# Attention values in four column quarters, and softmax sums added up by POOL and DVE

## The chip, the cores and the metric

One core of a Trainium2 chip runs the kernel. The metric is device time in microseconds (us) of one execution. A core has a matrix engine (TensorE, PE in the profile, with its weight loads as PEld), three engines for elementwise work (VectorE, DVE; ScalarE, ACT; GpSimd, POOL), and DMA queues, which the SyncE queue (SP) feeds here. Each engine works through its own queue in order; the queues wait for each other by semaphores. The matrix engine writes to PSUM, eight banks of 128 partitions by 512 fp32 numbers.

## The reference

Four layers with residuals: a gated recurrence, a feed-forward layer, a differential attention, the feed-forward layer again. The change is in the attention. Inputs: 2 sequences of 1024 tokens, width 512; 16 heads of 32, each with two query sets on the same keys and values.

```python
x = x + _L0_attn_b_ref(_layernorm(x), Wq1, Wq2, Wk, Wv, Wlam, Wo)

def _L0_attn_b_ref(x, Wq1, Wq2, Wk, Wv, Wlam, Wo):
    q1, q2, k, v = (split_heads(x @ W) for W in (Wq1, Wq2, Wk, Wv))
    q = concatenate([q1, q2], axis=1)
    scores = einsum('bhqd,bhkd->bhqk', q, repeat(k, 2)) / sqrt(d)
    p = softmax(where(causal, scores, finfo.min), axis=-1)
    y = einsum('bhqk,bhkd->bhqd', p, repeat(v, 2))
    lam = sigmoid(x @ Wlam)
    return (y[:, :H] - lam * y[:, H:]) @ Wo
```

## The kernel before

The work before and after the attention (the recurrence, lines up to 413, and the two feed-forward layers, lines 500 to 556) is untouched. Everything below is in the attention stage.

**Pairs.** A pair `(b, g, p, par)` is two heads of sequence `b` that are worked on together; index `e` (0, 1) tells the two apart. There are 32 pairs, in groups of four with the same `b` and `g`. The 1024 queries of a sequence are two halves `qb` of 512 (`BLK`), that is eight tiles of 128 (`P`); the 1024 keys are eight blocks `kb` of 128.

**Units.** Under the causal mask a half needs key blocks 0 to 3 or 0 to 7: twelve units `(qb, kb)` per pair, numbered 0 to 11 (`units`). Units 0 to 3 are the first half, 4 to 11 the second. A unit with `kb >= 4*qb` is on the diagonal: it needs only the last `BLK - lo` queries, with `lo` 0, 128, 256 or 384.

**Six steps.** A pair runs in six steps of two units each. In step `t` of pair `n` the matrix engine's order, written out by hand (`manual_schedule` for PE alone), is:

- `weights_step` (units 2t and 2t+1): scores `t` = keys x queries, transposed so that keys are the partitions (L858, four matmuls), then a product of 3 rows with ones that adds minus the maximum (L865, four matmuls). ACT takes the exponential into the weights tile `pr` (L873, four buffers, both heads in one tile); POOL zeroes the masked triangle of a diagonal unit (`affine_select`, L876).
- `weigh` for the two units of the step before: the product of values and weights (L895), accumulated in the one PSUM bank outside the ring (`edge_bank`).
- work listed in `beside` for this step: projections of a later group (L717), transposes of the maxima, and around the change of sequence the values, the division by the sums and the output projection.
- `maxima_step` of the next pair: scores with queries as partitions (L798), to which DVE adds the causal mask (L804) and whose maximum it takes (L808). Both orders of the scores are needed, for the maxima must be known before the exponentials.

The maxima of a pair are split into three bf16 parts by POOL (`split_maxima`, L825 to L829: first half of the queries at step 2 of the pair before, second half at step 0 of the pair itself, after DVE has taken the smaller of two partial results, L822) and turned by PE (`turn_maxima`, L836, copied by DVE, L838) one step later.

Scores, projections and turned maxima share a ring of seven PSUM banks (`ring_bank`). The queues of DVE, ACT, POOL and SP are ordered by the framework's scheduler when the program is built; the matrix engine's is not.

**The product with the values.** Values are kept with 33 columns a head (`HV`): 32 numbers and a one, so that row 32 of the product is the sum of the weights. A product takes 64 columns (33 of use), so the two heads take the two halves of the array's columns:

```python
nc.tensor.matmul(
    y[64 * e : 64 * e + 64, lo:],
    all_values[:, HV * (NH * kb + h) : HV * (NH * kb + h) + 64],
    pr[:, e, : BLK - lo], start=(kb == 0), stop=last,
)
```

After the last unit of a half ACT copies the bank to `ys` (L912); SP sends 32 rows a head to `shares` and one row a head to `totals`. At the end of a sequence `divide` takes reciprocals of `totals` and `combine` multiplies them in; `project_out` follows.

**Loads.** Queries and keys go through DRAM scratch and come back as `qs` (1024 queries of one head, six buffers) and `ks`, loaded for pair n+2 at step 1 of pair n.

## Time and profile before

| | |
|---|---|
| three runs | 2176.17, 2178.66, 2180.66 us (median 2178.66) |
| profiled execution | 2177.11 us |
| its span | 2175.3 us |
| granted PE clock, mean | 0.995 |
| PE busy | 2122.4 us (98%) |
| DVE, ACT, POOL busy | 1126.2, 837.3, 448.1 us |
| attention stage, first to last L865 | 844 to 1767 us |
| product with the values, L895 | 1536 records, 291.6 us busy |

An fp32 product shows as two records. Busy time counts overlapped records once. Records of a matmul have modelled ends, so the cost of a group of matmuls is read from its start to the start of the next group. The profile gives, for each engine, busy time and what ended its idle time.

### The profile page before, as it was taken

What the parts mean: (1) busy time and instruction counts of PE and PEld (TensorE: products, weight loads), DVE (VectorE), ACT (ScalarE), POOL (GpSimd) and SP (SyncE); (2) the same over time, 40 slices, a digit from 0 to 9 for tenths busy, and PEclk for the clock granted to TensorE, in tenths of its full rate; (3) what the DMA queues carried; (4) which work ended last, traced back from release to release, by engine and by line L of the source; (5) the groups of instructions that cost most, each with busy time, mean ns of one, the idle gap of its engine ahead of it and who ended that gap; (6) DMA issues with size and microseconds to landing.
All of it is one profiled execution on the core that took longest, in us unless ns stands there. A gap on an engine that the chain in (4) does not pass through costs nothing.

```text
span 2175.3 us, 26073 instructions
## 1 busy us (share of the span) xinstructions
PE 2122.4 (98%) x9072; PEld 1273.5 (59%) x9072; DVE 1126.2 (52%) x2056; ACT 837.3 (38%) x1592; POOL 448.1 (21%) x808
## 2 busy tenths in 40 slices
PE   8999999999999999999999999999999999999998
PEld 3444444688888844555555454454545547888887
DVE  4767676533443235565656574565656763333322
ACT  4344343234334322343444332243434533343433
POOL 0312123122122220111111112121212221222222
PEclk9999999999999999999999999999999999999999
DMA  6111211600000144343434341244443223000000
GB/s 251 58 58 58 88 58 73 246 1 1 1 1 1 35 105 106 98 112 87 121 83 119 76 123 41 73 104 106 104 105 88 64 83 160 0 20 20 1 20 20
DMA packets 77874, 161.41 MB, mean 74 GB/s; under 512 B 19376, under 2 KB 27568, under 8 KB 77744
## 3 DMA queue, kind: packets, MB, share of 16 engines
q1 hardware_dynamic: 77744, 159.75, 25.1%
q8 instruction: 73, 1.20, 0.2%
q14 instruction: 57, 0.47, 0.1%
HBM read 109.08 MB, written 41.94 MB: 69 GB/s over the span
## 4 chain that ended last, share of the span: by engine, by line
PE 86%; DVE 4%; DMA 4%; ACT 2%; SPq 2%; issue 2%; POOL 0%; DVEq 0%; ACTq 0%; POOLq 0%
PE y L895 11%; PE g L511 11%; PE u L511 11%; PE f_out L532 11%; PE t L858 6%; PE s L798 5%; PE ag L260 5%; PE kv L260 5%; PE pq L717 4%; PE pq L260 3%; PE pv L689 3%; PE a_out L408 3%; PE b_out L956 2%; DMA qs<-sc 2%; PE t L865 2%
## 5 line engine op out<-in xcount | busy, mean ns | idle before, releaser
L873 ACT ACTIVATE pr<-t 128x512 f32<-128x512 f32 (+3 forms) x768 | 314.8, 497 | 368.6 <-PE t L865 364.8
L808 DVE TENSOR_REDUCE nmax<-s 128x1 f32<-128x512 f32 (+3 forms) x640 | 369.7, 627 | 54.6 <-PE s L798 54.5
L895 PE MATMUL y<-pr,val 128*64 128x512 f32 (+3 forms) x1536 | 291.6, 501 | 0.8 <-POOL maxima L827 0.8
L526 POOL TENSOR_TENSOR ssq<-ssq,sq 128x512 f32<-128x512 f32 x120 | 155.9, 1299 | 602.5 <-ACT sq L525 602.5
L517 DVE TENSOR_TENSOR h<-h,u 128x512 f32<-128x512 f32 x128 | 88.0, 688 | 362.5 <-PE u L511 356.4
L511 PE MATMUL g<-xs,w 128*128 128x512 f32 x1024 | 261.8, 397 | 0.9 <-ACT xs L461 0.7
L532 PE MATMUL f_out<-w,hs 128*128 128x512 f32 x1024 | 257.7, 394 | 0.3 <-DVE hs L520 0.3
L511 PE MATMUL u<-xs,w 128*128 128x512 f32 x1024 | 257.0, 393 | 0.0
L876 POOL TENSOR_SCALAR_AFFINE_SELECT pr<-pr 128x256 f32<-128x256 f32 x256 | 101.4, 408 | 593.6 <-ACT pr L873 593.3
L858 PE MATMUL t<-qs,ks 128*128 128x512 f32 (+3 forms) x768 | 198.4, 357 | 22.1 <-DVE parts L729 9.6
L511 PEld LDWEIGHTS u<-xs,w 128*128 128x128 f32 x1024 | 192.9, 188 | 43.6
L532 PEld LDWEIGHTS f_out<-w,hs 128*128 128x128 f32 x1024 | 191.6, 188 | 43.9 <-DVE hs L520 1.1
L804 DVE TENSOR_TENSOR s<-s,causal 128x128 f32<-128x128 f32 (+1 forms) x384 | 115.3, 336 | 195.3 <-PE s L798 195.3
L511 PEld LDWEIGHTS g<-xs,w 128*128 128x128 f32 x1024 | 190.5, 188 | 43.9 <-ACT xs L461 0.9
L798 PE MATMUL s<-ks,qs 128*128 128x512 f32 (+3 forms) x768 | 206.9, 391 | 6.2 <-DMA sc<-parts 3.9
L858 PEld LDWEIGHTS t<-qs,ks 128*128 128x128 f32 x768 | 139.2, 188 | 78.2 <-issue 20.8
L717 PE MATMUL pq<-b_xt,w_qk 128*128 128x512 f32 x384 | 175.8, 603 | 0.0
L519 ACT CAST hs<-h 128x512 fp32r<-128x512 f32 x128 | 79.4, 621 | 237.5 <-DVE h L517 237.5
L895 PEld LDWEIGHTS y<-pr,val 128*64 128x64 f32 x1536 | 93.3, 136 | 120.2 <-issue 86.1
L516 ACT ACTIVATE h<-g 128x512 f32<-128x512 f32 x128 | 76.6, 598 | 224.0 <-PE g L511 223.9
L798 PEld LDWEIGHTS s<-ks,qs 128*128 128x128 f32 x768 | 115.0, 190 | 69.4 <-issue 58.6
L520 DVE TENSOR_TENSOR hs<-h,hs 128x512 fp32r<-128x512 f32 x128 | 88.6, 692 | 83.1 <-ACT hs L519 83.1
(151 smaller groups left out, 2145.5 us busy)
## 6 DMA issues: line engine op xcount, KB each, us to landing
qs<-sc SPq DMA_DIRECT2D x128, 256.0 KB, 4.9
w<-w_kept SPq DMA_DIRECT2D x32, 768.0 KB, 8.9
sc<-parts SPq DMA_DIRECT2D x384, 64.0 KB, 1.7
ks<-sc SPq DMA_DIRECT2D x128, 128.0 KB, 4.0
w_kept<-w SPq DMA_DIRECT2D x16, 768.0 KB, 3.2
w<-in_w_gu_dram SPq DMA_DIRECT2D x32, 256.0 KB, 2.8
share<-ys SPq DMA_DIRECT2D x128, 64.0 KB, 2.0
w_in<-in_w_in_t_dram SPq DMA_DIRECT2D x5, 1024.0 KB, 11.0
```

The lines of the kernel that those rows point to most:

```text
L260: nc.tensor.matmul(po, w[:, k, ts(c, P)], xt[:, k, :], start=(k == 0), stop=(k == NKC - 1))
L511: nc.tensor.matmul(po, ws[f][:, part, ts(k, P)], xs[:, e, k, :], start=(k == 0 and e == 0), stop=(k == NKC - 1 and e == 1),)
L526: nc.gpsimd.tensor_add(ssq, ssq, sq)
L532: nc.tensor.matmul(po[j], hp[:, e, ts(j, P)], ws[f][:, 2, :], start=(f == 0 and e == 0), stop=(f == NF - 1 and e == 1),)
L717: nc.tensor.matmul(po, w[:, k, ts(kind, P)], xts[b][:, k, ts(e, BLK)], start=(k == 0), stop=(k == NKC - 1),)
L798: nc.tensor.matmul(po[:, x, :], qs[:, ts(j, P)], ks[:, first : first + nk], start=True, stop=True,)
L804: nc.vector.tensor_tensor(diagonal, diagonal, causal.unsqueeze(1).to_broadcast([P, len(heads), P]), ALU.add,)
L808: nc.vector.tensor_reduce(nmax[pair][:, first // BLK, j, heads[0] : heads[-1] + 1], po, AX.X, ALU.max, negate=True,)
L858: nc.tensor.matmul(banks[u, e][:, :nq], ks[:, ts(kb, P)], qs[:, q0 : q0 + nq], start=True, stop=False,)
L873: nc.scalar.activation(pr[:, e, :nq], banks[u, e][:, :nq], AF.Exp)
L876: nc.gpsimd.affine_select(out=pr[:, :, :P], in_=pr[:, :, :P], compare_op=ALU.is_ge, fill=0.0, base=0, pattern=[[0, 2], [1, P]], channel_mu ...
L895: nc.tensor.matmul(y[64 * e : 64 * e + 64, lo:], all_values[:, HV * (NH * kb + h) : HV * (NH * kb + h) + 64], pr[:, e, : BLK - lo], start= ...
```

## The change

**Quarters.** The two heads' products are split once more, by the parity `a` of the query tile: even tiles go to columns 64a + 32e with a = 0, odd ones with a = 1. Each product uses the 32 values of a head as weights and half of the query tiles as the moving side, so four products fill the four quarters of the array's columns, and the output has 256 columns in place of 512. A diagonal unit with d tiles masked leaves out tiles below d, and the last one (d = 3) has odd tiles only.

**Sums.** The column of ones is gone, and so is the padding. The sums of weights are added up elementwise over key blocks in an fp32 tile `acc` per half: units 5 to 8 of the second half (the ones with `lo` = 0 after the first) by POOL, one add of both heads' 1024 numbers a partition each; the units with `lo` > 0 by DVE (1, 2, 3 and 9, 10, 11), with a copy of 2 x 128 numbers at unit 1. Unit 0 and unit 4 are read where they are, as the first term. `add_up` then multiplies `acc` by a matrix of ones for four blocks at once (two heads of this pair's first half, two of the last pair's second half) into one ring bank, ACT copies it, SP sends four rows to `totals`. It stands at step 2 of a pair, and once more after the last.

**Loads.** `qs` is two tiles, one per half, with four and six buffers, loaded for pair n+2 at step 2 of pair n and at step 0 of pair n+1.

**Room and order.** Two instead of four buffers of `maxima`, three instead of four of `mt`; the second half's `combine` and the output projection around the change of sequence come up to two steps later.

```diff
-        all_values = b_d.tile([P, NQ * NH * HV + 64 - HV], F32, name="val")
+        val = b_d.tile([P, NQ, D], F32, name="val")
+        ones32 = b_c.tile([P, HD], F32, name="ones32")
...
-        def load_stacks(pair):
+        def load_stacks(pair, halves=range(2)):
             b, g, p, par = pair
-            for e in range(2):
-                if par == 0:
-                    load_stack(b, g, 2, 2 * p + e)
-                load_stack(b, g, par, 2 * p + e)
+            for half in halves:
+                for e in range(2):
+                    if par == 0 and half == 0:
+                        load_stack(b, g, 2, 2 * p + e)
+                    load_stack(b, g, par, 2 * p + e, half)
...
                 steps.append((pair, u, pr))
+                if kb == 0:
+                    first_pr = pr
+                    continue
+                if kb == 1:
+                    accs[pair, qb] = b_a.tile(
+                        [P, 2, BLK], F32, tag=f"acc{qb}", name=f"acc{name(pair)}_{qb}"
+                    )
+                acc = accs[pair, qb]
+                more = first_pr if kb == 1 else acc
+                other = nc.vector if lo else nc.gpsimd
+                if kb == 1 and lo:
+                    other.tensor_copy(acc[:, :, :lo], more[:, :, :lo])
+                other.tensor_add(acc[:, :, lo:], more[:, :, lo:], pr[:, :, :nq])
             return steps
+        def add_up(*blocks):
+            n_sums[0] += 1
+            po = ring_bank(f"sums{n_sums[0]}")
+            rows = slice(0, 64 * len(blocks))
+            for x, (pair, qb) in enumerate(blocks):
+                for e in range(2):
+                    nc.tensor.matmul(
+                        po[64 * x + 32 * e :][:32], ones32, accs[pair, qb][:, e, :],
+                        start=True, stop=True,
+                    )
+            sm = b_c.tile([P, BLK], F32, tag="sums", name=f"sm{n_sums[0]}")
+            nc.scalar.copy(sm[rows], po[rows])
...
         def weigh(pair, u, pr):
...
-            for e in range(2):
-                h = operands(pair, e)[2]
-                nc.tensor.matmul(
-                    y[64 * e : 64 * e + 64, lo:],
-                    all_values[:, HV * (NH * kb + h) : HV * (NH * kb + h) + 64],
-                    pr[:, e, : BLK - lo],
-                    start=(kb == 0), stop=last,
-                )
+            for a in range(2):
+                first = a if a >= d else a + 2
+                if first < d:
+                    continue
+                for e in range(2):
+                    h = operands(pair, e)[2]
+                    nc.tensor.matmul(
+                        y[64 * a + 32 * e :][:32, first // 2 * P : 2 * P], val[:, kb, ts(h, HD)],
+                        pr[:, e, :].rearrange("p (t q) -> p t q", q=P)[:, first - d : QB - d : 2, :],
+                        start=(kb == 0), stop=(d == 2 + a),
+                    )
...
             if n + 2 < len(pairs):
-                at(n, 1, load_stacks, pairs[n + 2])
+                at(n, 2, load_stacks, pairs[n + 2], (0,))
+                at(n + 1, 0, load_stacks, pairs[n + 2], (1,))
...
+            at(n, 2, add_up, (pair, 0), *([(pairs[n - 1], 1)] if n else []))
...
                         for c in range(NKC):
-                            at(n + 1, 2 + 2 * e + c // 2, combine, b, c, e)
+                            m, t = ((n + 1, 2 + c // 2), (n + 1 + c // 2, 5 * (c < 2)))[e]
+                            at(m, t, combine, b, c, e)
                     for j in range(NQ):
-                        m, t = (n + 1, 5) if j < 2 else (n + 2, (j - 2) // 3)
+                        m, t = (n + 1, 5) if j < 2 else (n + 2, j // 2 - 1)
                         at(m, t, lambda b=b, j=j: project_out(b, j, held["o", b]))
```

## The prediction

> **What bounds the kernel now.** First the page: busy times, and the chain that ended last.
>
> ```profile
> PE 2122.4 (98%) x9072; PEld 1273.5 (59%) x9072; DVE 1126.2 (52%) x2056; ACT 837.3 (38%) x1592; POOL 448.1 (21%) x808
> PE 86%; DVE 4%; DMA 4%; ACT 2%; SPq 2%; issue 2%; POOL 0%; DVEq 0%; ACTq 0%; POOLq 0%
> ```
>
> PE sets the time. The granted clock is 0.995, so no clock gate is in it. Next, busy time by stretch, one stretch a pair of the attention stage (from one L865 of step 0 to the next pair's).
>
> ```profile
> core 0: us, PE busy (x) PEld busy (x) DVE busy (x) ACT busy (x) POOL busy (x), PEclk, DMA share, GB/s
> 1065.00:1102.00 37.00, 35.71 (x161) 17.79 (x160) 17.36 (x37) 13.16 (x30) 5.23 (x18) 1.00 0.37 93
> 1102.00:1131.50 29.50, 28.56 (x145) 14.74 (x144) 17.01 (x41) 11.99 (x28) 5.29 (x18) 1.00 0.40 99
> 1665.50:1686.90 21.40, 21.29 (x129) 11.66 (x128) 15.16 (x36) 10.79 (x26) 5.23 (x18) 1.00 0.37 88
> ```
>
> The four columns after PE are weight load, DVE, ACT, POOL. A pair takes 37, 29.5 or 21.4 us, as it carries four, two or no projections. I call the last kind tight: 17 of the 32 (two in each of the first seven groups of four, three in the last), two of them 23.8 with transposes beside. In a tight pair PE has 0.1 us idle, but DVE is already 71% busy. Third, the timeline of that tight pair by engine: PE, then ACT, then DVE, then POOL. Columns: start, length (us), engine, line, operation.
>
> ```profile
> 1672.82 0.39 PE L865 MATMUL t<-mt_s,ones 3*128 3x512 bf16 x4
> 1673.15 0.87 PE L895 MATMUL y<-pr,val 128*64 128x256 f32 x8
> 1673.95 0.95 PE L798 MATMUL s<-ks,qs 128*128 128x128 f32 x4
> ...
> 1680.28 1.94 PE L895 MATMUL y<-pr,val 128*64 128x512 f32 x8
> 1682.14 0.86 PE L798 MATMUL s<-ks,qs 128*128 128x384 f32 x3
> ...
> 1673.31 2.07 ACT L873 ACTIVATE pr<-t 128x512 f32<-128x512 f32 x4 [3.38 <-PE t L865]
> ...
> 1671.60 2.47 DVE L808 TENSOR_REDUCE nmax<-s 128x1 f32<-128x512 f32 x4
> 1674.42 0.43 DVE L804 TENSOR_TENSOR s<-s,causal 128x256 f32<-128x256 f32 x1 [0.35 <-PE s L798]
> 1674.77 1.61 DVE L808 TENSOR_REDUCE nmax<-s 128x1 f32<-128x512 f32 x3
> 1678.48 0.42 DVE L838 COPY mt_s<-mt 128x512 bf16<-128x512 bf16 x1 [2.11 <-PE mt L836]
> ...
> 1667.20 0.41 POOL L876 TENSOR_SCALAR_AFFINE_SELECT pr<-pr 128x256 f32<-128x256 f32 x1 [3.41 <-ACT pr L873]
> 1672.94 0.22 POOL L825 CAST maxima<-nmax 128x8 bf16<-128x8 f32 x1 [2.52 <-DVE nmax L808]
> 1674.12 0.22 POOL L829 COPY maxima<-maxima 128x24 bf16<-128x24 bf16 x1
> ```
>
> To be seen: the y groups' cost, DVE's pitch (0.62 us for a 512-wide reduction), and that DVE's and POOL's idle gaps are waits for PE and ACT, in order. Last, the price of an add:
>
> ```profile
> L526 POOL TENSOR_TENSOR ssq<-ssq,sq 128x512 f32<-128x512 f32 x120 | 155.9, 1299 | 602.5 <-ACT sq L525 602.5
> L520 DVE TENSOR_TENSOR hs<-h,hs 128x512 fp32r<-128x512 f32 x128 | 88.6, 692 | 83.1 <-ACT hs L519 83.1
> ```
>
> **PE's part.** From start to the next start, a y group of 512+512 columns takes 1.86 us and one of 256+128 takes 0.80: 1.66 ns a column and 0.16 fixed. Per pair and head 4608 columns pass in each half now. In quarters, the busier tile parity passes 2560 (12 units: 256 each, but 128 for the last two of either half). That removes 2048 x 1.66 = 3.39 us a pair; the six fixed parts stay. The sums add 512 columns, 0.85 us (1.01 if they stand apart from y). Net -2.54, times 32: -81 us. The trace shows two column halves at once, never four quarters: from no gain in y (3.39 dearer) to all of it; I take all of it, since two f32 streams start 7 ns apart and cost one, and the four row strips of L865 start within 10 ns.
>
> The Trainium skill (TensorE: Matmul & The Clock Gate, Part 3) gives 2.38 times for three column tiles of 32. If four did no better, a pair's y would pass 2 x 4608/2.38 = 3870 column times, an estimate, and 2.2 us of the 3.39 would be lost. No run here shows it.
>
> **DVE's part.** Per pair a copy of 256 elements and six adds of 768, 512, 256, twice. At the reduction's pitch of 0.62 and 1.04 ns an element: 0.25 + 2(0.89+0.62+0.36) = 4.0 us (3.4 by elements alone, 4.4 by the unpipelined means). DVE goes from 15.2 to 19.2 us a tight pair.
>
> **POOL's part.** Four adds of 1024 elements (units 5 to 8). L826's 8 elements take 0.21, L526's 512 take 1.30: 2.39 each on a line (2.33 if they grow as the memsets do, 0.53 to 0.94; 2.60 doubled). 9.6 us; POOL goes from 5.2 to 14.8.
>
> By busy sums a tight pair would take PE's 18.9 or DVE's 19.2 us. But the queues are in order, and the built order of the changed kernel puts these in series:
>
> 1. POOL's queue: four adds (units 5, 6, 7, 8), the select of unit 8 before the last add, the select of unit 9 after it. The first add needs the exponentials of unit 5. PE's y of unit 9 needs that last select: 9.6 + 0.8 = 10.4 us after the exponentials. From step 2 to step 5 PE takes 10.5 us now, less 1.06 for the shorter y groups and sums: 9.5, and 0.6 to that y, less 2.56 for the exponentials: it would come after 7.5. PE is 2.9 us late by this alone.
> 2. DVE's add of unit 9 waits for the same select. Queued behind it: two of step 4's three reductions, all of step 5, and the next pair's steps 0 and 1. PE waits for those through its 7 score banks.
> 3. At each pair's start DVE's copy of unit 0 and add of unit 1 stand before the first reduction of step 0, and unit 3's second score takes that reduction's bank. Exponentials of unit 1 end 2.34 us after step 0's L865; select, 0.15 + 0.41; add 0.89; reduction 0.5; the score 0.15: step 1 starts at 4.5, not 2.85 (3.06 now, less 0.21 of y). PE stalls 1.65 us in every pair, backlog or not.
>
> The loop of a tight pair, from select 9 to the next select 9: DVE does its whole pair work but steps 2 and 3 (1.96 + 2.55), the start of step 4 (0.9) and the last three reductions of step 1 (1.86): 15.16 - 7.27 + 4.0 = 11.9. That frees the bank for unit 5's last score: 0.23 to step 2, 2.56 to the end of unit 5's exponentials (1672.82 to 1675.38), 0.15 to POOL. Then 10.4 on POOL, 0.1 to DVE. Sum 25.3 us against 21.4: **+3.9, times 17: +66 us.** The split of the maxima ends earlier (after two reductions and 1.4 us) and is covered.
>
> In pairs with projections the added PE work covers POOL's chain. 37 us pairs: -2.54 + 1.65 = -0.9. In the 29.5 us pairs a projection's DVE step and step 4's reductions stand behind add 9 too: between -0.9 and +0.8; I take 0. Seven of each: -6. The last pair has no maxima for DVE, but POOL's chain of 10.4 where PE leaves 8.1 now: +2.
>
> The other edits: query loads in halves carry the same bytes by twice the DMAs; SP moves the first half past a step's scratch and share DMAs (needed some 12 us later), the second is issued at a pair's step 0 behind the share DMAs and needed at step 1. Median landing is 4.9 us now; with step 1 at 4.5 or later it is covered, in an unstalled pair it would cost up to 2. Each sums copy stands on ACT before step 3's exponentials: 0.6 us, covered by PE's scores. Fewer maxima and mt buffers, the later combine and project_out: nothing, PE has other work there; the divide of a batch's second half may hold DVE for a 2 us landing once.
>
> Sum against the profiled execution's 2177.1 (median of the runs 2178.7): 2177.1 + 66 - 6 + 2 = **2239**.
>
> DVE and POOL already hold each other up in this trace: three L526 adds that began with 0.5 us of an L520 add still running took 1.67 to 1.68 us instead of 1.30. The skill (SBUF — State Buffer, Who interferes with whom) says that a DVE instruction with two SBUF inputs and a GpSimd one that reads SBUF exclude each other for a whole instruction, which speaks against splitting one sum between them. Each of the six DVE adds may meet a select (0.41): 0 to 2.5 us a tight pair, 0 to +42 in all; I take 0, for most reductions read PSUM.
>
> **Rivals.**
> A, faster: the chain on POOL is hidden and PE alone decides, 2177 - 81 = 2096. For it: all busy sums are under 19.3. It decides if a 1024-wide add takes under (7.5 - 0.8)/4 = 1.7 us, and DVE's waits find other banks. Against it: 1.30 us for half the width.
> B, quarters run two at a time, so the change does not do what it says: +3.39 in 14 pairs with projections, some 1 us in tight ones: 2239 + 47 + 17 = 2303.
> C, no backlog on DVE (items 1 and 3 only): a tight pair takes 18.9 + 1.65 + 2.9 = 23.45; 2177 + 35 - 13 + 2 = 2201.
> D, the exclusion counts in full: 2281.
>
> **Chances.** Forecast 0.48, A 0.13 (0.02 of it no change), B 0.09, C 0.15, D 0.15. POOL's price alone moves the forecast by -5 to +14, DVE's by -9 to +7. The range 2190 to 2305 leaves out A and the upper half of B. A measurement of this kernel can tell about 0.2%, 4.4 us, from no change: faster 0.11, same 0.02, slower 0.87.
>
> **What would show it.** POOL adds near 2.4 us; tight pairs near 25 us with PE waiting for POOL's selects and DVE's reductions; y groups of 512+512 columns near 1.0 us; DVE busy near 19 us a pair but idle in front of add 9. Tight pairs at 19 to 21 us would prove it wrong, y groups at 1.8 us would prove B.

## The result, and the profile after

The changed kernel takes 2363.9 us, the median of four runs (2361.1 to 2367.8); the kernel before took 2178.1 beside it (2176.2 to 2180.7). The ratio is 1.085, with a 95% interval of 1.083 to 1.087. The forecast of 2239 had the direction, and missed the size by 125 us; its range ended at 2305.

First the page of after: engine rows, the granted clock by slices of the span (in tenths), the chain of work that ended last, followed back from the last instruction, and three rows of groups.

```profile
PE 2173.1 (92%) x10598; PEld 1318.1 (56%) x10608; DVE 1264.8 (53%) x2280; ACT 841.3 (36%) x1625; POOL 773.8 (33%) x933
PEclk9999999999999999988898899988988889999999
PE 67%; POOL 9%; DVE 9%; issue 4%; DMA 4%; ACT 3%; SPq 2%; DVEq 0%; POOLq 0%; ACTq 0%
L935 PE MATMUL y<-pr,val 128*32 128x256 f32 (+1 forms) x2816 | 210.6, 380 | 47.3 <-POOL pr L875 47.3
L893 POOL TENSOR_TENSOR acc<-acc,pr 128x1024 f32<-128x1024 f32 x96 | 227.5, 2370 | 29.0 <-ACT pr L872 23.9
L893 DVE TENSOR_TENSOR acc<-acc,pr 128x512 f32<-128x512 f32 (+2 forms) x160 | 112.4, 702 | 142.5 <-POOL pr L875 140.8
```

The clock's row before:

```profile
PEclk9999999999999999999999999999999999999999
```

PE's share of the chain fell from 86% to 67%, and POOL and DVE hold 18%. PE's busy time **rose**, from 2122.4 to 2173.1, although it has less work. The second row says why: slices of the attention stage carry an 8, where all carried a 9 before. The mean granted clock is 0.943 against 0.995.

Next the busy time by stretch: a pair with four projections, one with two, and three tight pairs (columns as in the forecast's fence; the number before DMA share is the granted clock).

```profile
1104.50:1148.00 43.50, 38.43 (x213) 19.19 (x212) 22.14 (x47) 13.32 (x31) 14.78 (x22) 0.88 0.26 67
1148.00:1186.30 38.30, 31.28 (x193) 16.42 (x192) 21.80 (x48) 12.15 (x29) 15.32 (x22) 0.87 0.38 104
1657.00:1683.40 26.40, 21.43 (x177) 12.30 (x176) 17.94 (x39) 10.85 (x27) 16.00 (x22) 0.95 0.29 76
1683.40:1710.10 26.70, 21.20 (x181) 12.16 (x180) 19.06 (x42) 10.85 (x27) 15.44 (x22) 0.95 0.36 95
1819.60:1848.50 28.90, 24.14 (x181) 14.16 (x180) 20.06 (x45) 10.86 (x27) 15.45 (x22) 0.80 0.25 69
```

The last two do the same work, with the same order of instructions on every engine, and one takes 2.2 us longer: the longer one has the lower clock. Over 15 tight pairs the mean is 27.3 us (21.4 before), over six pairs of the 37 us kind 43.4 (37.4), over six of the 29.5 us kind 37.0 (29.5). So the pairs that the forecast let go free, those with projections, lost as much as the tight ones and more.

The waits of PE in the attention stage, longest first:

```profile
PE t L857 <- DVE nmax L808: 59.7, 49, 2.7
PE y L935 <- POOL pr L875: 47.3, 34, 2.0
PE t L857 <- DVE parts L727: 33.2, 13, 2.6
PE s L798 <- DMA qs<-sc: 14.1, 12, 2.1
```

Two of these had a counterpart before:

```profile
PE t L858 <- DVE parts L729: 9.6, 14, 1.0
PE t L858 <- DVE nmax L808: 4.7, 16, 0.9
```

The first two waits of after are, in the main, the forecast's items 3 and 1. The third is new in size: 13 of the 14 pairs with projections lose 2.5 us each. In the pair from 1104.50 it looks like this, PE first, then DVE (L727 is DVE's step of a projection):

```profile
1138.26 0.47 PE L857 MATMUL t<-qs,ks 128*128 128x128 f32 x1 [2.55 <-DVE parts L727]
...
1136.25 0.96 DVE L893 TENSOR_TENSOR acc<-acc,pr 128x768 f32<-128x768 f32 x1 [5.36 <-POOL pr L875]
1137.52 0.68 DVE L727 SCALAR_TENSOR_TENSOR parts<-pq,parts 128x512 fp32r<-128x512 f32 x1
```

DVE's addition of unit 9 waits for POOL's select (the zeroing of the masked triangle), and the projection's step, which frees a bank for PE, stands behind it. And the timeline of the tight pair from 1657.00, PE first, then POOL, then DVE:

```profile
1661.28 0.30 PE L857 MATMUL t<-qs,ks 128*128 128x128 f32 x1 [1.45 <-DVE nmax L808]
...
1670.60 1.07 PE L935 MATMUL y<-pr,val 128*32 128x256 f32 x16
1671.60 0.40 PE L836 MATMUL mt<-ident,maxima 128*128 128x128 bf16 x4
...
1677.18 0.84 PE L935 MATMUL y<-pr,val 128*32 128x256 f32 x12 [0.74 <-POOL pr L875]
1679.97 0.63 PE L935 MATMUL y<-pr,val 128*32 128x256 f32 x4 [1.95 <-POOL pr L875]
...
1660.06 0.80 POOL L826 TENSOR_TENSOR mrest<-nmax,maxima 128x8 f32<-128x8 f32 x1
...
1669.11 2.39 POOL L893 TENSOR_TENSOR acc<-pr,pr 128x1024 f32<-128x1024 f32 x1 [1.05 <-ACT pr L872]
1671.92 4.84 POOL L893 TENSOR_TENSOR acc<-acc,pr 128x1024 f32<-128x1024 f32 x2 [0.42 <-ACT pr L872]
1676.72 0.41 POOL L875 TENSOR_SCALAR_AFFINE_SELECT pr<-pr 128x256 f32<-128x256 f32 x1
1677.21 2.35 POOL L893 TENSOR_TENSOR acc<-acc,pr 128x1024 f32<-128x1024 f32 x1
...
1679.95 1.13 DVE L893 TENSOR_TENSOR acc<-acc,pr 128x768 f32<-128x768 f32 x1 [3.61 <-POOL pr L875]
```

This is the forecast's chain as it was written: four additions in a row on POOL (but for 0.42 us in which the second waits for unit 6's exponentials) with the select of unit 8 before the last, PE's values of units 8 and 9 late by 0.74 + 1.95 = 2.7 us (2.9 forecast), PE's score at the pair's start late by 1.45 (1.65 forecast). A y group of 512+512 columns takes 1.00 us from start to start (1670.60 to 1671.60), 1.86 before: the four quarters run at once, and rival B is out.

**An account of the 190.7 us** that the span grew. PE's idle time (span less busy) went from 52.9 to 192.9: +140. Its work at full clock fell by 2.0 us a pair (e9 below), 64 us in all. The rest, 115, should then be half clock. The trace's clock record has 48 stretches of half clock in the stage (counted from 860 to 1940 us), 33 of them of 3.41 us and the others of two, four or five times that, 239 us together. PE was busy in 227 us of them, and half of that, 113, is what full speed would have saved. I call this the half-clock loss; between the same marks it was 0 before. Each stretch follows a window of 3.41 us in which PE was busy for 21 to 80% (median 40%); the longest single gap of PE in such a window was 0.4 to 2.6 us. Windows with no drop behind them had 56% or more, so between 56 and 80% the share alone does not decide.

So the missing term is named by subtraction, and the clock record has it in size. That does not yet show that it cost time: where a pair waits for POOL and DVE, a slower PE could just use up its own waits. That is what the runs had to tell.

### The profile page after: what moved, and what is told of

It is laid out like the page before. It is cut to its first block, busy times and chain, and to the rows that moved or that the text cites. A ratio compares the mean times of both kernels' runs of the same rounds, so it can differ in the third digit from the quotient of the medians.

```text
span 2366.0 us, 29917 instructions
## 1 busy us (share of the span) xinstructions
PE 2173.1 (92%) x10598; PEld 1318.1 (56%) x10608; DVE 1264.8 (53%) x2280; ACT 841.3 (36%) x1625; POOL 773.8 (33%) x933
## 4 chain that ended last, share of the span: by engine, by line
PE 67%; POOL 9%; DVE 9%; issue 4%; DMA 4%; ACT 3%; SPq 2%; DVEq 0%; POOLq 0%; ACTq 0%
PE g L511 10%; PE u L511 10%; PE f_out L532 10%; POOL acc L893 7%; PE pq L715 6%; PE t L857 5%; PE y L935 4%; PE s L798 4%; PE kv L260 3%; PE ag L260 2%; PE pv L687 2%; PE t L864 2%; PE b_out L990 2%; ACT pr L872 2%; DVE acc L893 1%
## 5 line engine op out<-in xcount | busy, mean ns | idle before, releaser
L857 PE MATMUL t<-qs,ks 128*128 128x512 f32 (+3 forms) x768 | 222.4, 392 | 96.9 <-DVE nmax L808 59.7
L798 PE MATMUL s<-ks,qs 128*128 128x512 f32 (+3 forms) x768 | 237.4, 425 | 19.1 <-DMA qs<-sc 16.4
L935 PE MATMUL y<-pr,val 128*32 128x256 f32 (+1 forms) x2816 | 210.6, 380 | 47.3 <-POOL pr L875 47.3
L857 PEld LDWEIGHTS t<-qs,ks 128*128 128x128 f32 x768 | 156.0, 212 | 160.4 <-issue 67.3
L893 POOL TENSOR_TENSOR acc<-acc,pr 128x1024 f32<-128x1024 f32 x96 | 227.5, 2370 | 29.0 <-ACT pr L872 23.9
L511 PEld LDWEIGHTS u<-xs,w 128*128 128x128 f32 x1024 | 192.3, 188 | 43.4
L875 POOL TENSOR_SCALAR_AFFINE_SELECT pr<-pr 128x256 f32<-128x256 f32 x256 | 113.8, 460 | 278.9 <-ACT pr L872 211.5
L715 PE MATMUL pq<-b_xt,w_qk 128*128 128x512 f32 x384 | 204.2, 683 | 0.0
L893 DVE TENSOR_TENSOR acc<-acc,pr 128x512 f32<-128x512 f32 (+2 forms) x160 | 112.4, 702 | 142.5 <-POOL pr L875 140.8
L798 PEld LDWEIGHTS s<-ks,qs 128*128 128x128 f32 x768 | 128.5, 206 | 106.4 <-issue 70.9
```

Source lines behind the costliest of these rows:

```text
L511: nc.tensor.matmul(po, ws[f][:, part, ts(k, P)], xs[:, e, k, :], start=(k == 0 and e == 0), stop=(k == NKC - 1 and e == 1),)
L715: nc.tensor.matmul(po, w[:, k, ts(kind, P)], xts[b][:, k, ts(e, BLK)], start=(k == 0), stop=(k == NKC - 1),)
L798: nc.tensor.matmul(po[:, x, :], qs[j // QB][:, ts(j % QB, P)], ks[:, first : first + nk], start=True, stop=True,)
L857: nc.tensor.matmul(banks[u, e][:, :nq], ks[:, ts(kb, P)], qs[qb][:, lo:], start=True, stop=False,)
L893: other.tensor_add(acc[:, :, lo:], more[:, :, lo:], pr[:, :, :nq])
L935: nc.tensor.matmul(y[64 * a + 32 * e :][:32, first // 2 * P : 2 * P], val[:, kb, ts(h, HD)], pr[:, e, :].rearrange("p (t q) -> p t q", q=P ...
```

## The experiments

Times are medians. Idle is span less PE's busy time over the whole run, and loss the half-clock loss between 860 and 1940 us, worked out as above; both are of the profiled execution, which is within some 5 us of the median except in e3 (2273).

| run | us | PE idle | loss |
|---|---|---|---|
| before | 2178 | 53 | 0 |
| after | 2364 | 193 | 113 |
| e1 no additions | 2188 | 91 | 38 |
| e2 none on POOL | 2244 | 113 | 69 |
| e3 none on DVE | 2264 | 138 | 77 |
| e4 fill | 2356 | 132 | 31 |
| e5 sums first | 2363 | 193 | 107 |
| e6 additions later | 2342 | 188 | 107 |
| e8 fitted fill | 2295 | 126 | 15 |
| e9 no additions, early queries | 2112 | 49 | 5 |
| e10 after, early queries | 2344 | 181 | 102 |
| e11 dealt out, early queries | 2244 | 123 | 42 |
| e12 dealt out, late queries | 2291 | 136 | 83 |
| e13 unit 9 to POOL | 2245 | 130 | 47 |
| e14 e11 in written order | 2201 | 110 | 25 |
| e15 e13 in written order | 2182 | 104 | 14 |
| e16 e6 in written order | 2321 | 188 | 76 |
| e17 batch ones on DVE | 2177 | 97 | 15 |
| e18 units 10, 11 to POOL | 2182 | 98 | 22 |
| e19 sums last | 2159 | 81 | 10 |

**e1, e2, e3: leave additions out.** e1 drops the whole block from `if kb == 0` to `other.tensor_add` in `weights_step` and reads a fixed tile; e2 begins the second half's sum at unit 8; e3 keeps POOL's four only.

> All twelve additions of a pair are left out; the product with ones reads a fixed tile of ones, so the sums are not those of the reference. Everything else is as after. Theory (the idle time of the forecast was right, 193 us of PE idle after against 53 before; the missing 113 to 132 us are TensorE's half clock, which begins in 3.41-us windows that follow a wait of PE): without the additions no wait arises, so the stage shows no stretch of half clock worth more than some 5 us, and PE's work is smaller by the forecast's 2.54 us in each of 32 pairs: 2177 - 81 = 2096 us, 2080 to 2120. Rival (products in column quarters, or their weight loads, are slower than the forecast took them): 2177 or more even without an addition. Rival (the half loads of the queries come late): PE still waits some 14 us for them, 2110 to 2130.

> POOL's four additions of a pair are left out: the second half's sum begins with units 8 and 9, so its sums lack units 4 to 7 (1.0 is added to each instead); DVE's additions stay. Theory: the waits for POOL's weights before the values (47 us in 34 waits) and POOL's wait for the sums in the loose pairs go; what stays is DVE's queue at the start of a pair (1.65 us by the forecast, 60 us in 49 waits for the shift in the trace after). Without half clock 2096 + 32 x 1.65 = 2149 us; a wait of 1 to 2 us a pair may still drop the clock in some, up to 50 us more: 2140 to 2200. Rival (DVE's own load of 19 us a pair is what bounds): 2250 or more.

> DVE's additions and its copy are left out: the first half's sum is a fixed tile of ones, the second half's holds units 5 to 8 added to ones, by POOL in four additions as before. Theory: the waits for POOL before the values of units 8 and 9 stay (2.9 us in each of 17 tight pairs by the forecast, so 2096 + 49 = 2145 us) and the half clock with them (17 x 1.7 us): some 2180 us, 2140 to 2210; waits for DVE's shift are gone. Rival (only additions of both engines together disturb, by the port they share): 2100 to 2110.

e1 took 2188.3 (ratio 1.005): without an addition the change still gains nothing. The theory fell. The first rival has the time (2177 or more) but not the reason, for e1's tight pairs without a wait take 19.4 us, 2.0 less than before. The waits of e1 in the stage name the reason; it is that of the second rival, with three times the wait.

```profile
PE s L798 <- DMA qs<-sc: 42.7, 23, 3.6
PE t L857 <- DVE parts L727: 8.6, 13, 0.7
```

The maxima's products wait 43 us in 23 places for the half loads of the queries, where after had 14 us. I had expected 14, because I read a wait that stands behind other waits as its full price. (A pair has ten additions and a copy, not the twelve that the expectation names.) e2 took 2243.8 and e3 2263.9, 44 and 54 us above their ranges, since these were counted from 2096. Counted from e1 they are 56 and 76 us, where the ranges had 44 to 104 and 44 to 114: the waits for DVE's reductions stayed in e2 (57 us) and those for POOL in e3 (49 us), as expected, with losses of 69 and 77. So DVE's additions cost 56 us over e1, POOL's 76, both together 176. The 56 is a net figure: e3 still waits 43 us for queries, as e1 does, but e2 only 7.

**e9 and e10: load the second halves of the queries early.**

```diff
-                at(n, 2, load_stacks, pairs[n + 2], (0,))
-                at(n + 1, 0, load_stacks, pairs[n + 2], (1,))
+                at(n, 2, load_stacks, pairs[n + 2])
```

> The kernel without additions (its sums are read from a fixed tile of ones), with both halves of the queries of the pair after next loaded at step 2, in place of the second half at step 0 of the next pair. Without this the kernel without additions took 2188, with 43 us of waits for these loads in 23 places and 38 us lost to half clock. Theory (the second halves are issued too late, one step before their use): these waits fall under 10 us, half clock under 10 us of loss: 2177 - 64 (the work that PE saves by the tight pairs of that run, 21.4 to 19.4 us) = 2113, up to 2135 us. Rival (the transfers themselves are slow, by their number or their size): the waits stay over 25 us, 2165 or more.

> After, with both halves of the queries loaded at step 2, two pairs ahead, as in e9, where this took 76 us from the kernel without additions. The trace after has 14 us of waits for these loads in 12 places, all in pairs with projections. Theory (each such wait costs its own length and then half clock, about as much again, as in e1 with 38 us of idle time and 35 us of half clock): 14 to 40 us less, 2324 to 2350 us. Rival (the waits for DVE and POOL behind them take their place, as the pair's loop sets the time): 2355 or more.

e9, which is e1 with this edit, took 2111.7: the waits for queries are gone, and so is the half clock but for 5 us of loss. 77 us went for 43 us of waits; 33 of the 77 are half-clock loss. The stretch of one tight pair of e9:

```profile
1605.00:1624.40 19.40, 19.40 (x182) 11.59 (x176) 15.19 (x36) 10.85 (x28) 5.22 (x18) 1.00 0.42 116
```

PE is busy all the time at full clock, so 19.40 against 21.40 is the work that the change saves: 2.0 us a pair where the forecast had 2.54. In after the same edit (e10) gives 20 us, for 14 us of waits.

**e4 and e8: fill PE's waits with products that nobody reads.** The queues that PE waits for keep their work; only PE is not idle meanwhile. e8's edit, with a like one (two products) ahead of unit 9's values in pairs with `p == 1`, nearly all of them tight:

```diff
+                    if (u, e) == (3, 0):
+                        for _ in range(2):
+                            nc.tensor.matmul(banks[2, 0][:, 256:512], ident, val[:, 0, 0:256],
+                                             start=False, stop=False)
+                    if (u, e) == (11, 1) and pair[2] == 0:
+                        for _ in range(4):
+                            nc.tensor.matmul(outs[pair][:, 256:512], ident, val[:, 0, 0:256],
+                                             start=False, stop=False)
```

> After, with products added that nobody reads (128x128 by 256 columns of 4-byte values, about 0.43 us each at full clock) where PE waits: three ahead of unit 3's second score, one ahead of unit 8's values, three ahead of unit 9's. They take no wait away and add 3 us of work a pair, laid into waits of 1.5 to 2.9 us. Theory (half clock after the waits costs 113 to 132 us of the 187): the stretches of half clock become much fewer in spite of the added work, and the time falls to 2250 to 2290 us. Rival (the half clock goes with the waits but costs nothing of its own, or does not come from PE's idle time): 2364 us or more, as the added products cost up to 96 us.

> After, with products added that nobody reads, this time sized to the waits: two (1.1 us) ahead of unit 3's second score in every pair, two ahead of unit 9's values in pairs without projections, four (2.3 us) ahead of unit 11's second score in pairs with projections, where the trace after has waits of 1.4 to 2.1, 1.9 and 2.5 us. The e4 run had 14 such instructions (4.0 us) in every pair and took 2356: there PE's half-clock loss fell by 81 us and its idle time by 61, but 128 us of products were added, more than the waits held. Theory (half clock follows the waits, and is a cost of its own): with some 80 us of products inside the waits the loss by half clock falls from 113 to under 50 us, and tight pairs all take some 26.4 us (27.3 on average after), pairs with projections 4 us less than after: 2280 to 2315 us. Rival (the pairs are set by the loop through DVE and POOL, and a slower PE only uses up its own waits): 2350 or more.

e4 missed both of its expectations: the loss fell from 113 to 31 as the theory has it, but each product took 0.57 us and not 0.43, PE's work grew by 128 us, and where the waits were shorter than the fill it stood on the path. e8, with the fill sized to the waits, took 2294.9, inside its range: **some 90 us of useless work were added (PE's busy time less its work and its loss), and the kernel became 69 us faster.** Two stretches of e8, a tight pair and one of the 37 us kind:

```profile
1603.70:1629.20 25.50, 22.27 (x185) 12.76 (x184) 18.58 (x42) 10.85 (x27) 15.96 (x22) 1.00 0.32 91
1088.50:1126.90 38.40, 36.37 (x225) 19.49 (x224) 23.13 (x49) 13.32 (x31) 15.43 (x22) 1.00 0.29 77
```

The clock is 1.00 in both. The tight pair takes 25.5 us, the forecast's loop was 25.3; the other takes 38.4 where after took 43.5. One thing besides the fill differs: in 15 pairs the framework ordered DVE's queue a little differently (the addition of unit 1 later). The gain does not hang on that: the 17 pairs with the same order on DVE as in after became 32 us shorter and lost 41 us less by half clock. With this the half clock is shown to be a cost of its own, and not only a sign of waiting. It also shows how the two terms hang together: the chain that the profile follows back through e8's tight pairs is the forecast's loop, from DVE's addition of unit 9 (1626.62) through additions and reductions on DVE to a score of unit 5 (1638.84; 12.2 us, forecast 11.9), and over POOL's additions and selects to the next addition of unit 9 (1652.66). It was sized right, for a PE at full clock.

**e5, e6, e16: move things in after's queues.** e5 puts `add_up` first in step 2, ahead of the projection; e6 collects the additions and issues them behind `maxima_step`; e16 is e6 with POOL's queue in program order (selects, chain of the maxima, additions).

> After, with the products with ones placed first in step 2, ahead of the projection and the maxima of that step. Nothing else differs. Theory (in the pairs with projections POOL's first addition of a pair waits for these sums, because the second half's sum has one buffer, and so its chain, DVE's addition of unit 9 and the projection's shift behind that are all late): the 14 pairs with projections, 37 to 43 us on average after, become 3 to 6 us shorter, the tight ones stay: 2364 - 42 to 84 = 2280 to 2322 us. Rival (their excess comes from half clock and DVE's queue at the pair's start alone): no more than 10 us from after, 2354 to 2374.

> After, with every addition placed in the program behind the maxima of its step, so that DVE has the reductions of step 0 before its copy of unit 0 and its addition of unit 1. POOL's order is the same. Theory (the stall at a pair's start is that queue): the waits of scores for DVE's shift, 60 us in 49 waits after, shrink to under 15 us, and half clock with them; the waits for POOL stay. 2364 - 45 to 90 = 2275 to 2320 us. Rival (the loop through POOL's chain and DVE's addition of unit 9 sets the pair, and a later addition only moves the wait): 2350 or more.

> As e6 (after, every addition behind the maxima of its step), with POOL's queue in the written order: the selects of units 8 and 9 now stand ahead of the addition of unit 8, so unit 9's values wait for three additions (7.1 us) and not four (9.5). DVE's addition of unit 9 still waits for the addition of unit 8. Theory of the forecast (the loop of a tight pair runs over POOL's four additions, DVE's addition of unit 9 and the reductions behind it): the waits of the values, 44 us in e6, go, but the pair is not shorter by more than 1 us, 2320 to 2345 against e6's 2342. Rival (PE's own wait at the values of unit 9 is what counts, with its half clock): 30 us and as much again less, 2260 to 2300.

e5 took 2363.0, the rival's figure: the theory fell. POOL's wait for the sums was real, and went (after first, then e5):

```profile
POOL acc L893 <- PE sums L906: 90.8, 14, 11.1
```

```profile
POOL acc L893 <- PE sums L906: 15.3, 4, 7.7
```

But PE's wait for the projection's step on DVE stayed (34.5 us in 15 places): in the pair from 1144.9 of e5 the first addition of POOL comes 14.8 us after the pair's start, not 20.3, and the next one then waits 4.6 us for its exponentials, so that it is only 1.7 us earlier. Pairs of the 29.5 us kind gained 1.9 us each, those of the 37 us kind nothing, and other pairs lost what was gained. A wait of 9 us on an engine was worth next to nothing, because the chain behind it was set by a later arrival. e6 took 2341.7, between its two expectations (2320 and 2350): the waits for reductions fell from 60 to 18 us, and others took their place (19 us before the sums for DVE's additions, 32 for queries). Pairs of the 37 us kind gained 4.3 us, tight ones lost 0.7. e16 took 2321.2: tight pairs 25.0 after e6's 28.0, the waits of the values 44 to 21 us, but a new stall of 12 us at the change of batch that its written order makes (e15 shows it). With that stall it lies at the lower edge of the first expectation (2320 to 2345), but tight pairs became 3.0 us shorter where that allowed 1, and half of the values' waits stayed. So how much of item 1 is PE's own wait and how much the loop is not settled in after's own queues.

**e11, e12, e13: deal the additions out.** POOL takes units 1, 2, 3, 5, 7, DVE 6, 8, 9, 10, 11; queries early. e12 has the queries late; e13 gives unit 9 to POOL.

```diff
-                other = nc.vector if lo else nc.gpsimd
+                other = nc.gpsimd if u in (1, 2, 3, 5, 7) else nc.vector
```

> After, with the additions dealt out differently: POOL adds units 1, 2, 3, 5 and 7 (with the copy of unit 0), DVE units 6, 8, 9, 10 and 11; queries loaded early as in e10. POOL now has two 1024-wide additions (2.37 us each) and no more than one of them ahead of the select of unit 8, in place of four around the selects of units 8 and 9; DVE's queue at a pair's start holds no addition. DVE's own load stays near 19.4 us in a tight pair (15.2, two 1024-wide additions of some 1.2, and 0.96 + 0.70 + 0.41), PE's is 19.4. Theory (the order of the additions, not their number, makes the waits, and the waits make the half clock): tight pairs take 19.5 to 21.5 us, the others 0 to 1.5 us more than without additions: 2112 + 0 to 55 = 2112 to 2167 us, faster than before. Rival (DVE has no room for it: at 19.4 of 19.4 us its backlog holds PE's banks, or it and POOL hold each other up over 32 times 1.5 us): 2180 or more.

> The additions dealt out as in e11, with the queries loaded in after's places. Theory (late second halves cost 76 us where PE has no other wait, as between e1 and e9): 60 to 80 us above e11. Rival (they cost no more than the 14 us that they take in after): under 30 us above e11.

> As e11, with unit 9's addition (768 elements) moved from DVE to POOL, which gets 1.8 us a pair, DVE loses 0.96 us. If DVE's load is what holds e11 back, this is 10 to 40 us below e11; if it is POOL's queue ahead of the selects of units 10 and 11, it is above e11; if neither, within 10 us of it.

e11 took 2244.2, 100 us less than e10 and 77 above its range: the rival's figure. Where a pair starts PE waits again, in the pair from 1073.4 for 2.4 us, and the timeline of DVE, and then of POOL, shows what stands there.

```profile
1075.97 0.42 DVE L804 TENSOR_TENSOR s<-s,causal 128x256 f32<-128x256 f32 x1
1076.30 1.76 DVE L822 TENSOR_TENSOR nmax<-nmax 128x8 f32<-128x8 f32 x1
1077.99 0.42 DVE L804 TENSOR_TENSOR s<-s,causal 128x256 f32<-128x256 f32 x1
```

```profile
1076.24 1.80 POOL L893 TENSOR_TENSOR acc<-pr,pr 128x768 f32<-128x768 f32 x1
1078.13 0.22 POOL L825 CAST maxima<-nmax 128x8 bf16<-128x8 f32 x1
```

In before the same minimum was this:

```profile
1666.64 0.17 DVE L822 TENSOR_TENSOR nmax<-nmax 128x8 f32<-128x8 f32 x1
```

A minimum of eight elements, 0.17 us there, lasts 1.76 us: it ends 0.02 us after POOL's addition, which began 0.06 us before it. Each has two inputs in SBUF. POOL's second row is the other effect: the chain of the maxima, for which PE's transposes wait, stands behind that addition. e12 is 47 us above e11, between its two expectations; e13 is level with e11.

**e14, e15: write POOL's order out.** In each step the selects, then the chain of the maxima, then the additions, DVE's too. DVE instead of POOL writes the zeros of the factors, four times in all.

```diff
-        ordered.enter_context(tc.manual_schedule(engines={mybir.EngineType.PE}))
+        ordered.enter_context(
+            tc.manual_schedule(engines={mybir.EngineType.PE, mybir.EngineType.Pool})
+        )
...
-                made = weights_step(pair, step)
+                made, later = weights_step(pair, step)
...
+                for f, *args in later:
+                    f(*args)
```

> As e11 (the additions dealt out, queries early), with POOL's queue in a written order: in each step first the selects of its two units, then the chain of the maxima, then the additions of the step (the zeros of the factors are written by DVE instead, four times in all). In e11 POOL's addition of unit 1 stood ahead of the maxima's chain: PE's transposes waited 26 us in 18 places for it, and DVE's minimum of 8 elements, which is 0.16 us otherwise, took 1.76 us while that addition ran. Theory (order alone, and DVE and POOL holding each other up over two inputs in SBUF, makes e11's 132 us above the kernel without additions): both waits shrink, half clock with them, and tight pairs take 19.8 to 21.5 us (24.3 on average in e11): 2130 to 2180 us. Rival (DVE's and POOL's loads as such are too much): within 20 us of e11's 2244.

> As e14, with unit 9's addition on POOL instead of DVE. If the two engines' holding each other up matters more than DVE's load, it is within 10 us of e14; if DVE's load matters, 10 to 30 us below; if POOL's queue ahead of the selects of units 10 and 11 does, above.

e14 took 2200.8, 43 us less than e11 with the same additions on the same engines, and e15 19 us less again, 2181.7, as expected where DVE's load matters. So order (POOL's, DVE's additions behind the maxima, and the four small writes on DVE) was worth a third of the 132 us that e11 still lost against e9. e14 ends 21 us above its range; 12 of these are a stall that I had not foreseen, at the change of batch, here in POOL's waits of e15:

```profile
POOL tot L946 <- DVE factors L969: 32.4, 1, 32.4
```

POOL, now in program order, stands before the write of a table that DVE still reads, and PE's transposes lose 12.2 us behind it.

**e17, e18, e19.** e17 lets DVE write that table, e18 gives POOL units 10 and 11 too, and e19 puts `add_up` behind the maxima of step 2.

> As e15, with the ones that a batch's table of sums starts from written by DVE too. In e15 POOL, now in a written order, stood 32 us before that write in one place (at the change of batch), and PE's transposes 12.2 us behind it, with a stretch of half clock. Theory (the additions, in this order, cost under 2.5 us in a tight pair and next to nothing in the others): 2181.7 - 12 to 15 = 2167 to 2170 us, faster than before by 0.4 to 0.6%. Rival (DVE stalls there instead, or the wait turns up elsewhere): 2178 or more.

> As e17, with the additions of units 10 and 11 on POOL too, 1.28 + 0.73 us a pair there for 0.68 + 0.42 on DVE. In e15 DVE's two stand in the first steps of a pair ahead of the reductions for which PE waits 0.9 and 0.4 us. If that is what is left, tight pairs fall from 21.6 to 20.5 and the time is 10 to 20 us below e17; if POOL's queue ahead of the selects of units 0 and 1 and of the maxima's chain is nearer the edge, it is 10 us or more above e17.

> As e18, with the products with ones behind the maxima's products of step 2 instead of ahead of them, about 1 us later on PE. In e18 PE waits 29 us in 19 places for POOL's additions of units 2 and 3 ahead of these products, 1.34 us in each tight pair. Theory (what is left in a tight pair is where a result is asked for, not the additions' load): 0.95 us less in each of 17 tight pairs and fewer stretches of half clock: 2155 to 2170 us, faster than before by 0.4 to 1%. Rival (POOL's queue is full, and its addition of unit 5, which waits for the same products, only moves the wait to the next select): 2178 or more.

e17 took 2177.4, a ratio of 0.9997 (0.9988 to 1.0006): level with before. It missed its range by 7 us and lies just under its rival's bound, as the pair at the change of batch still takes 91.3 us (86.0 before) with 10.2 us of half clock in it. e18 took 2182.4, 5 us more and between its expectations: it moved the waits rather than taking them away, for reductions 31 to 14 us, for POOL before the sums 11 to 29. e19 then asked for the sums one group of products later, and took **2159.4, inside its range, a ratio of 0.9914 (0.9901 to 0.9928)**: faster than both kernels. Its page, one of its tight pairs, and PE's longest waits:

```profile
PE 2076.7 (96%) x10598; PEld 1268.7 (59%) x10608; DVE 1209.4 (56%) x2126; ACT 843.4 (39%) x1625; POOL 867.4 (40%) x1087
```

```profile
1700.70:1722.10 21.40, 19.92 (x177) 11.25 (x177) 17.60 (x37) 10.95 (x27) 17.58 (x28) 1.00 0.07 14
```

```profile
PE sums L906 <- POOL acc L1109: 13.6, 17, 3.7
PE t L857 <- DVE nmax L808: 12.3, 32, 1.1
```

Tight pairs take 21.0 us on average (21.4 before), those of the 37 us kind 35.7, those of the 29.5 us kind 27.5. POOL is busy in 17.6 of 21.4 us, so I take this deal of the additions to be near its end.

## Why the forecast was right in sign and wrong in size

- **PE's part, -2.54 us a pair: mis-sized.** It is -2.0 (e9). From start to next start the y groups of a tight pair take 5.39 us in e9, 8.65 before (-3.26, forecast -3.39), the sums 0.97 (forecast 0.85), and the scores 0.27 more than before, which the forecast left out. In 32 pairs that is 17 us of the miss.
- **"The granted clock is 0.995, so no clock gate is in it": the step that failed.** It read the clock of a kernel whose PE had 0.1 us of idle time in a tight pair, and carried it to a kernel for which the same text implied 6.5 us of idle time there. The term that it put at nothing is 113 us by the account (the profiled execution missed the forecast by 129), and e8 got 69 us of time back by keeping PE busy in the waits, with some 90 us of filling products. The Trainium skill (TensorE: Matmul & The Clock Gate, Why this matters for your kernels) asks for no gaps of PE over some 3 us; the measurement differs: the longest single gap in a window ahead of a drop was 2.6 us, and in 32 of the 48 it was under 2 us.
- **Tight pairs, 25.3 us: right at full clock.** e8's take 25.5 at best, 26.1 on average; after's 27.3, with 2.9 of half-clock loss. POOL's addition (2.37 us, forecast 2.39; the line through the forecast's two prices gives 2.41), item 1 (2.7, forecast 2.9) and item 3 (1.45, forecast 1.65) were as forecast.
- **Pairs with projections, -6 us in 14 pairs: wrong.** "The added PE work covers POOL's chain" holds for PE's own waits, but not for DVE's queue: the projection's step stands behind the addition of unit 9, and PE waits 2.5 us for it. The forecast named this for the 29.5 us pairs alone and took 0 for it; it came in pairs of both kinds. Item 3's stall and the queries come on top. Twelve of these pairs lost 6.0 or 7.5 us each, 81 us, some 58 of it half-clock loss (5.1 and 4.6 us a pair more than before).
- **PE's idle time agrees by accident.** The forecast implies 143 us more of it (66 - 6 + 2 + 81), and 140 came; but tight pairs have 4.9 us where 6.5 were implied, since a slow PE fills its own waits, and pairs with projections have 3.4 to 5.4 more where 1.65 to 2.5 were.
- **Query loads, "covered, up to 2 in an unstalled pair": too low.** In after they cost 20 us (e10); without the additions 77 (e9).
- **DVE and POOL, rival D priced at 0.** They do hold each other up (L822 in e11, and in after POOL's L826, 0.80 us instead of 0.21 in 14 places), as the Trainium skill has it (SBUF — State Buffer, Who interferes with whom). The selects' mean of 460 ns against 408 before sums to 13 us, mostly off the path. What it cost after in all was not measured by itself; in e11 it was one of two things that e14's order took away.
- **Rivals.** A's condition, a hidden chain on POOL, is not met by after, but its arithmetic is nearly that of e9: 2112, not 2096. B is refuted by the 1.00 us of a y group. C (2201) had no backlog on DVE, where after's DVE stood 146 us in front of its additions, waiting for POOL's selects. D's mechanism is there, but its 2281 has no half clock either.

Left open: how item 1's cost in after divides between PE's own wait and the loop (e16), and why the pair at the change of batch takes 5 us more than before in e17 and e19.

## What to carry to other kernels

When a change turns a full PE into one that waits, price each wait twice: its length, and the half clock that may follow it. In these runs the second was about as large as the first where waits were long (113 to 140 in after, 38 to 38 in e1, 69 to 60 in e2, each against the idle time that was added), and a quarter to a half of it where a tight pair had some 2 us of idle time and not 5 (14 to 51 in e15, 25 to 57 in e14). When work moves to POOL or DVE, write down their queues in order and ask of each entry who waits behind it: the same ten additions cost 232 us over e9 as first placed (e10) and 48 us as placed in e19. And do not read a wait's price from a trace where other waits hide it: late loads with 14 us of waits in after cost 77 us once the rest was gone.

## What the runs showed of the hardware

- Four f32 products in the four column quarters of the array, each with 32 columns of weights, run at once: in after they start 7 ns apart, and 512+512 columns of two heads take 1.00 us, where two halves took 1.86. The Trainium skill (TensorE: Matmul & The Clock Gate, Part 3) has 2.38 times for three column tiles; per column this is about four times (2048 column passes in 0.84 us beyond the fixed 0.16, at 1.66 ns each for one at a time).
- TensorE's clock falls to half in steps of 3.41 us after windows in which PE was busy for 21 to 80% of the time (after), not only after idle ones. Of after's 249 such windows at full clock a bound of 54% busy puts 6 on the wrong side, and a bound of 1.15 us for the longest single gap 8; these traces do not say which of the two counts. Keeping PE busy with products that nobody reads brought the mean granted clock from 0.943 back to 0.990 (e8).
- A DVE instruction of 0.17 us with two inputs in SBUF lasted 1.76 us beside a POOL addition of 1.80 us (e11).
